# Group statistics summed ahead on ScalarE at the head, and half 1's second modes rewritten

## The chip, the cores and the metric

The kernel runs on one core of a Trainium2 chip. Its metric is the device time of one execution in microseconds (us); of several executions the median counts. Five engines work beside each other, each with an instruction queue of its own: TensorE (PE, with its weight loads as PEld), VectorE (DVE), ScalarE (ACT), GpSimd (POOL) and SyncE (SP). SP only issues DMAs here; ACT and POOL issue some too. Sixteen DMA engines serve the core.

## The reference

Two layers work on x, 256 x 256 pixels of 128 channels in float32; both first normalize x by group statistics and both add their result to x.

```python
x = x + _L0_conv_ref(_gn(x), ...)   # attention along each row of pixels, 4 heads, gated
x = x + _L1_conv_ref(_gn(x), ...)   # 256 tokens of 256 x 128 pixels

def _gn(v, G=32, eps=1e-5):
    g = v.reshape(B_, H_, W_, G, C_ // G)
    m = jnp.mean(g, axis=(1, 2, 4), keepdims=True)
    s = jnp.var(g, axis=(1, 2, 4), keepdims=True)
    return ((g - m) / jnp.sqrt(s + eps)).reshape(v.shape)
```

Layer 0's first normalization needs the mean and variance of all of x before the first row can be computed. Layer 1 attends between tokens and then applies two spectral layers in groups of four tokens: a forward transform of each image to 32 x 16 modes, a complex 4 x 4 mix of the modes with mix_wr and mix_wi, the inverse transform, instance norms, and between the two layers a gelu. What the document calls "second modes" is the part of the second spectral layer that works on modes: transform, mix, energy (for the norm) and the first step of the synthesis.

## The kernel before

**Head (layer0, lines 132 to 171).** A loop over 32 blocks loads x in pieces of 1 MB (tile xb, four buffers, L141), transposes each on PE into PSUM banks (L145; the pool has six) and lets DVE gather bn_stats of each bank (L146). After block 2 the loop asks for the weights (L153), whose transposes stand on PE in the order of the loop; after block 8 comes `prepare` (exponentials of the bias). Then one bn_aggr over all 128 pieces (L166), `group_stats` (L46 to 61: two matmuls with gavg, an evacuation on ACT after each, `rsqrt` with a Sqrt on ACT), and `fold` (L231), which scales the weights wq and wg by the result.

**Rows (Rows.run, L280).** One pass over 256 rows, with an order of PE, ACT, DVE, POOL and SP written out by hand. For a pair of rows `turn` transposes x and kv on DVE (L303) and asks for the pair after next; `project` computes queries and keys (L318 evacuates), `values` the values and the gate's input (L322 to 328), `gates` the tanh. `scores`, two exponentials (L352), a product with the bias on DVE for two heads (L368) and on POOL for the other two (L370), pair sums on POOL (L375), then `attend`. Row 0's projection, values and gate stand before the first scores.

**Half 1's second modes (second_modes with a = 1, L1729).** Tokens are worked on in two halves of 128. `first_images(1)` writes the transformed rows as 16 stores of 16 image rows each to Yd in DRAM, from POOL's queue (L1723). `second_modes` then loads Yd in pieces YT of 512 KB by chunk of modes and half of the rows (L1741), from SP, into two buffers (chunks 2 and 3 wait for 0 and 1); `forward` transforms a chunk (L1754) and copies it to F (L1760); `mix_modes` makes 32 products of 256 elements on DVE and POOL (L1505), each added up by a matmul with the identity (L1518), chunks 0 and 1 first; `mixed` copies the sums to Z; `norm` takes the energies (L1543) and an rsqrt; `synth_modes` makes each of four chunks in four banks (L689), copies them (L707, ACT and DVE in turn) and stores them to Gd2 from SP and ACT (L712), with two gt buffers. Its pools are opened after those of the stage before are closed. Meanwhile `Output1.ahead` loads y and x for four half blocks and sums them (ACT L1907, POOL L1911).

**Output of half 1 (Output1.run, L1913).** For each of 16 blocks: skip and image matmuls (L1322, L1307) from modes `gs` that SP loads from Gd2 (L1331), ACT evacuates (L1843), DVE adds x + y (L1849; for the later half blocks L1896 has made that sum), POOL stores (L1850). SP's queue holds, in this order: modes of four blocks, y and x of half blocks 4 to 7, then for each block the modes four ahead and y and x eight half blocks ahead. There are eight half-block buffers for x and five for y.

Of the kernel before, what the change touches and what calls it, by code (L numbers as in the profile page):

```python
# [10 lines left out]
FP = mybir.dt.float32  # L11
# [19 lines left out]
def rsqrt(nc, pool, out, var, eps, tag):  # L31
# [8 lines left out]
    nc.vector.tensor_mul(n, r, r)  # L40
    nc.vector.tensor_mul(n, n, ve)
# [65 lines left out]
def layer0(tc, I, C, ident, x1d, U, Q2, mv2, groups):  # L107
# [11 lines left out]
    with ExitStack() as ctx:  # L119
# [11 lines left out]
        rows = Rows(tc, I, rctx, x1d, U, Q2, mv2, wT, bg, adft, bad, ident)  # L131
        with tc.tile_pool(name="l0p", bufs=2) as pp, tc.tile_pool(
            name="l0pp", bufs=6, space=PSUM
        ) as ps_p:
            gavg = pp.tile([P, P], FP, name="gavg", bufs=1)
            stats = pp.tile([P, NS // 2, 6], FP, name="stats1", bufs=1)

            xr = x.rearrange("s q c -> (s q) c").rearrange("(b p n) c -> b p n c", p=P, n=16)
            for b in range(xr.shape[0]):
                xb = pp.tile([P, 16, P], FP, tag="xb", name=f"xb_{b}", bufs=4)  # L140
# [6 lines left out]
                if b == 2:  # L147
                    nc.sync.dma_start(gavg, C["gavg"])
                    nc.sync.dma_start(bg, I["L0_conv_bg"].unsqueeze(1))
                    nc.sync.dma_start(adft, C["adft"].rearrange("(j p) f -> p j f", p=P))  # L150
                    for n in ("wq", "wk", "wv", "wg", "wo"):
# [5 lines left out]
                        if n in ("wq", "wo"):  # L157
                            nc.scalar.mul(wT[n], ps[:, 0:P], WO_SCALE if n == "wo" else 1.0 / math.sqrt(32.0))
                        else:
                            nc.scalar.copy(wT[n], ps[:, 0:P])  # L160
                if b == 8:
                    rows.prepare(pp, ps_p)
            rows.load(0)
            rows.load(1)
            mv = pp.tile([P, 2], FP, name="mv1", bufs=1)
            nc.vector.bn_aggr(mv, stats.rearrange("p a b -> p (a b)"))  # L166
            g = group_stats(nc, pp, ps_p, mv, gavg, "g1")
            nc.vector.tensor_copy(mr, g)
            rows.fold(ps_p, mr)

        rows.run()
# [35 lines left out]
class Rows:  # L207
# [23 lines left out]
    def fold(self, psum, mr):  # L231

        nc = self.tc.nc
        nc.vector.tensor_scalar(self.nm, mr[:, 0:1], -1.0, None, ALU.mult)
        ps = psum.tile([P, 512], FP, tag="a", name="foldps")
        for k, n in enumerate(("wq", "wg")):
            nc.vector.tensor_scalar(self.wn[n], self.wT[n], mr[:, 1:2], None, ALU.mult)
            nc.tensor.matmul(ps[:, k : k + 1], self.wn[n], self.nm, start=True, stop=True)
        nc.vector.tensor_copy(self.qb, ps[:, 0:1])
        nc.vector.tensor_scalar(self.hbg, ps[:, 1:2], self.bg, 0.5, ALU.add, ALU.mult)  # L240
# [39 lines left out]
    def run(self):  # L280
# [4 lines left out]
        wk = ctx.enter_context(tc.tile_pool(name="l0wk", bufs=2))  # L285
        ps_s = ctx.enter_context(tc.tile_pool(name="l0s", bufs=1, space=PSUM))
        ps_a = ctx.enter_context(tc.tile_pool(name="l0a", bufs=4, space=PSUM))
        pairs = {}
        turned = wk.tile([P, 6, 512], FP, name="turned", bufs=1)
# [19 lines left out]

        def project(s):  # L310
            p, q = row(s)
            ps = ps_a.tile([P, 512], FP, tag="a", name=f"qk_{s}")
            by_columns(ps[:, 0:256], self.wn["wq"], p["xT"][:, q])
            by_columns(ps[:, 256:512], wT["wk"], p["kvT"][:, q])
            r = rows[s] = {}
            r["qkT"] = wk.tile([P, 512], FP, tag="qkT", name=f"qkT_{s}")

            nc.scalar.activation(r["qkT"], ps, AF.Identity, bias=self.qb)  # L318

        def values(g):  # L320
# [4 lines left out]
            p["v"] = wk.tile([P, 4, P], FP, tag="v", name=f"v_{g}")  # L325
            nc.scalar.copy(p["v"].rearrange("p c d -> p (c d)"), ps)
            p["g"] = ps_a.tile([P, 512], FP, tag="a", name=f"g_{g}")
# [134 lines left out]

        with tc.manual_schedule(engines={ENG.PE, ENG.Activation, ENG.DVE, ENG.Pool, ENG.SP}):
            turn(0)
            for i in range(-1, NS + 1):
# [4 lines left out]
                if not odd and whole(g):  # L470
                    gates(g)
# [4 lines left out]
                if 0 <= i < NS:  # L476
# [3 lines left out]
                    weigh(i)  # L480
                if odd and whole(g + 1):
                    values(g + 1)
                if odd and whole(g + 2):
                    turn(g + 2)
# [151 lines left out]
def layer1(tc, I, C, ident, x1d, upool, U, Q2, groups, out):  # L636
# [9 lines left out]
    with ExitStack() as ctx:  # L646
# [983 lines left out]
        def first_images(a, wp, yp, psk, pst, first=None):  # L1630
# [44 lines left out]
            for b in range(17):  # L1675
# [37 lines left out]
                if b > 0:  # L1713
# [9 lines left out]
                    nc.gpsimd.dma_start(  # L1723
# [4 lines left out]

        def second_modes(a, wp, mk, psum, gts, yts):  # L1729

            h = halves[a]
            ym, yv, ra, lam, r2, rho, sig, _, kap, c0, hm, hv = (h.col[:, k : k + 1] for k in range(12))
# [29 lines left out]
            if a:  # L1762
                for hc in range(2):
                    for c in range(2):
                        load(c, (hc,))

                nc.scalar.activation(h.col[:, 12:13], yv, AF.Sqrt)
            else:
                load(0)
# [3 lines left out]
            load(2 if a else 1)  # L1773
            yield 4.0
            forward(1)
            if not a:
                load(2)
# [14 lines left out]
            for c in range(4):  # L1792
                if c == 2:
                    ps = psum.tile(f"cvps_{a}")
                    for i in range(4):
                        for r in range(2):
# [7 lines left out]
                            queues=(nc.sync if a else nc.gpsimd, nc.scalar))  # L1804
# [4 lines left out]
                if c == 1:  # L1809
                    run(tail)  # L1810

                    for i in range(4):
                        r = slice(32 * i, 32 * i + 32)
                        v = h.row[r, 0:P].rearrange("k (b d x) -> k b d x", b=2, d=2)
                        nc.vector.tensor_tensor(
                            h.bl0[r].rearrange("k (b d x) -> k b d x", b=2, d=2),
                            v[:, :: (-1 if i & 2 else 1), :: (-1 if i & 1 else 1)],
# [364 lines left out]
```

## Time and profile before

| | us |
|---|---|
| median of 3 runs | 2650.92 (2647.06 to 2656.12) |
| profiled execution, its own time | 2650.27 |
| its span on the core | 2648.5 |
| busy in the span: PE / DVE / POOL / ACT | 2406.1 / 2032.0 / 1485.6 / 1420.4 |
| input pass, to the end of the last bn_stats | 0 to 101.1 |
| rows begin: first product on POOL | 123.0 |
| last yA stored, second modes of half 1 begin | 2442.8 |
| last store of modes has landed | 2504.2 |

A line of the profile's timeline has the start, the duration, the engine, the line of the program, the operation, what it writes and reads, shapes, how many, and in brackets how long the engine had been idle before it and what ended that. A line of the chain of waits has start, length and the work that the end was waiting for. In the 40 slices each digit is a busy share in tenths, for PEclk the granted clock of TensorE in tenths.

### The profile page before, as it was taken

To read this page: it belongs to the slowest core of one execution; us is meant where nothing else is said; L and a number is where in the kernel's file an instruction comes from. 1 tells how busy PE (TensorE), PEld (TensorE's weight loads), DVE (VectorE), ACT (ScalarE), POOL (GpSimd) and SP (SyncE) were. 2 spreads that over 40 slices of the span, in tenths; PEclk is the share of its full clock that TensorE was granted. 3 is DMA by queue.
4 is the path that set the end of the run, shared out by engine and by line. 5 is a ranking of instruction groups with operands and counts; after the bars stand their busy time and mean duration, and the time that the engine had idled before them with its cause. 6 is when DMAs were issued, how large, how long until landed. Compare 5 with 4: busy or idle time off the path is not lost. (4 is left out here: it accounts for less than half of the span.)

```text
span 2648.5 us, 88789 instructions
## 1 busy us (share of the span) xinstructions
PE 2406.1 (91%) x37586; PEld 1537.2 (58%) x37586; DVE 2032.0 (77%) x2883; ACT 1420.4 (54%) x2720; POOL 1485.6 (56%) x1041
## 2 busy tenths in 40 slices
PE   6699999999999999999998999998979888898754
PEld 6555655555565656565554567786754466454522
DVE  7799999999999999999997457566646654465455
ACT  0278888888888888888885122001016402555232
POOL 1199999999999999999995012002136412111211
PEclk9899999999999999999998999999989988999855
DMA  9655566566565656566563011888877755997699
GB/s 360 215 92 101 105 107 107 103 107 106 105 106 100 111 100 109 103 106 106 105 107 70 6 58 63 268 273 289 296 278 268 261 194 159 333 349 268 196 384 350
DMA packets 1016869, 458.49 MB, mean 173 GB/s; under 512 B 831062, under 2 KB 946217, under 8 KB 1010072
## 3 DMA queue, kind: packets, MB, share of 16 engines
q1 hardware_dynamic: 976664, 362.61, 54.7%
q0 software_dynamic: 22912, 81.80, 8.0%
q10 hardware_dynamic: 16896, 8.39, 1.1%
q8 instruction: 298, 4.88, 0.8%
q14 instruction: 99, 0.81, 0.1%
HBM read 317.36 MB, written 135.27 MB: 171 GB/s over the span
## 5 line engine op out<-in xcount | busy, mean ns | idle before, releaser
L370 POOL TENSOR_TENSOR e<-e,b1T 128x1024 f32<-128x1024 f32 x255 | 604.4, 2370 | 145.8 <-DMA xk<-in_L_conv_kv_x_dram 78.5
L375 POOL TENSOR_TENSOR es<-e 128x512 f32<-128x512 f32 x512 | 648.0, 1288 | 0.1
L397 DVE RECIPROCAL av<-av 128x256 f32<-128x256 f32 x256 | 452.2, 1766 | 9.1
L352 ACT ACTIVATE sc<-sc,b2T 128x512 f32<-128x512 f32 x514 | 340.0, 662 | 123.9 <-PE sc L343 111.8
L352 ACT ACTIVATE e<-sc,b2T 128x512 f32<-128x512 f32 x510 | 322.8, 693 | 0.0
L368 DVE TENSOR_TENSOR e<-sc,b1T 128x1024 f32<-128x1024 f32 x257 | 312.1, 1215 | 10.1 <-ACT sc L352 9.7
L343 PE MATMUL sc<-qkT 32*128 32x256 f32 x4096 | 293.7, 400 | 2.5 <-DVE e L368 2.5
L1440 PE MATMUL yps<-xt,mpT 128*128 128x256 f32 x1024 | 246.5, 391 | 31.8 <-DMA xt<-x1d 16.0
L385 PE MATMUL av<-e,v 128*32 128x256 f32 x4096 | 268.6, 379 | 1.8 <-DVE gate L398 1.7
L343 PEld LDWEIGHTS sc<-qkT 32*128 32x128 f32 x4096 | 185.7, 184 | 114.9 <-issue 52.3
L1440 PEld LDWEIGHTS yps<-xt,mpT 128*128 128x128 f32 x1024 | 192.0, 193 | 76.1 <-DVE yt L1452 20.2
L385 PEld LDWEIGHTS av<-e,v 128*32 128x32 f32 x4096 | 130.2, 110 | 125.8 <-issue 38.1
L1456 POOL DMA_DIRECT2D yd<-yt x32 | 17.4, 545 | 317.0 <-DVE yt L1452 311.1
L318 ACT ACTIVATE qkT<-qk,qb 128x512 f32<-128x512 f32 x256 | 174.0, 680 | 6.6 <-PE qk L295 6.5
L295 PE MATMUL qk<-turned,wn_wq 128*32 128x256 f32 x2048 | 164.0, 392 | 1.8 <-DVE turned L303 1.8
L442 ACT ACTIVATE turned<-turned 128x256 f32<-128x256 f32 x256 | 104.3, 408 | 112.1 <-DVE x1b L410 109.8
L390 PE MATMUL av<-es,ones 128*32 128x256 f32 x2048 | 160.7, 379 | 1.6 <-POOL es L375 1.6
L295 PEld LDWEIGHTS u<-adft,x 128*32 128x32 f32 x4096 | 118.5, 110 | 74.9 <-issue 74.7
L295 PE MATMUL qk<-turned,wT_wk 128*32 128x256 f32 x2048 | 157.9, 380 | 0.0
L303 DVE STREAM_TRANSPOSE turned<-xk 128x1024 f32<-128x1024 f32 x128 | 157.8, 1233 | 0.1
L1843 ACT ACTIVATE blocks<-h2ps,col 128x512 f32<-128x512 f32 x128 | 88.8, 778 | 128.1 <-PE h2ps L1307 128.1
L295 PE MATMUL u<-adft,x 128*32 128x129 f32 x4096 | 137.0, 273 | 0.0
(544 smaller groups left out, 4163.8 us busy)
## 6 DMA issues: line engine op xcount, KB each, us to landing
xt<-x1d SPq DMA_DIRECT2D x128, 512.0 KB, 6.6
xb<-in_x_dram SPq DMA_DIRECT2D x32, 1024.0 KB, 7.8
xk<-in_x_dram SPq DMA_DIRECT2D x512, 64.0 KB, 3.2
xk<-in_L_conv_kv_x_dram SPq DMA_DIRECT2D x512, 64.0 KB, 2.8
x1d<-x1b SPq DMA_DIRECT2D x512, 64.0 KB, 2.3
x<-x1d SPq DMA_DIRECT2D x126, 256.0 KB, 3.2
y<-yd SPq DMA_DIRECT2D x62, 512.0 KB, 7.1
gs<-Gd SPq DMA_DIRECT2D x384, 64.0 KB, 5.4
```

The source lines that it names most:

```text
L295: nc.tensor.matmul(out[hd], w[:, hd], src, start=start, stop=stop)
L303: nc.vector.transpose(turned[:, a : b + 1 : b - a].rearrange("p k (b c) -> p k b c", c=32), t)
L318: nc.scalar.activation(r["qkT"], ps, AF.Identity, bias=self.qb)
L343: nc.tensor.matmul(sc[h // 2][:, h % 2, c * 256 : (c + 1) * 256], qkT[p, 256 + c * P : 256 + (c + 1) * P], qkT[p, 0:256], start=True, stop ...
L352: nc.scalar.activation(r["e"][1][:, :, c, :] if hp and s < NS - 1 else z, z, AF.Exp, bias=b2T[:, c, s : s + 1])
L368: nc.vector.tensor_tensor(e, sc.rearrange("p h x -> p (h x)"), w, ALU.mult)
L370: nc.gpsimd.tensor_tensor(e, e, w, ALU.mult)
L375: nc.gpsimd.tensor_tensor(es, e[:, :, 0, :], e[:, :, 1, :], ALU.add)
L385: nc.tensor.matmul(ps[hd, 0:256], p["v"][:, 2 * (s % 2) + c, hd], r["e"][h // 2][:, h % 2, c, :], start=(c == 0), stop=(c == 1),)
L390: nc.tensor.matmul(ps[32 * h : 32 * h + 32, 256:512], self.ones, r["es"][h // 2][:, h % 2, :], start=True, stop=True,)
L397: nc.vector.reciprocal(rd, rd)
L1440: nc.tensor.matmul(rows_of(ps[j]), mpT[:, sc, tt], by_turn(xt[:, sc])[:, j], start=(sc == 0), stop=False,)
```

## The change

*Head.* Blocks of x lie in five fixed places inside the tile U (free until the rows fill it) instead of four buffers; the pool of PSUM banks has four. After block 29 the statistics of the first 30 blocks are summed by ACT (three activations with accumulators) and finished by POOL; a Sqrt is issued behind them. After the last block bn_aggr takes only the last two blocks, and the matmuls with gavg add both parts, weighted by 30/32 and 2/32. `rsqrt` has one DVE operation fewer, the evacuations on ACT are gone. `Rows.run` is a generator now: pair 0 is turned and its keys are made before the rsqrt, row 0's queries after the fold of wq, and the gate of pair 0 after the first row's products.

*Half 1's second modes.* A class LastModes takes the place of second_modes(1). All of Yd is loaded into tiles of the pool xp: rows 0 to 127 in two loads, rows 128 to 223 in three, rows 224 to 255 in three. The last yA is stored from ACT's queue. The transforms of the first 128 rows run for all chunks, then those of the second; products are made in 16 groups of two, DVE's straight from PSUM, every third group on POOL, three buffers; PSUM banks are named by use. Synthesis goes 1, 0, 2, 3; all its stores are issued by SP. y and x are loaded for half blocks 0 and 1 ahead of the stores, for 2 and 3 behind the last; the sums are made on DVE.

*Output.* The x tiles hold whole blocks (three in xp, one in op), y has four buffers, gs five. The pools xp and head stay open. Elsewhere `shift` and `turned_blocks` hold what second_modes did in place, for both halves.

```diff
@@ layer0 @@
+steps = rows.run()
+next(steps)
 with tc.tile_pool(name="l0p", bufs=2) as pp, tc.tile_pool(
-    name="l0pp", bufs=6, space=PSUM
+    name="l0pp", bufs=4, space=PSUM
 ) as ps_p:
-    gavg = pp.tile([P, P], FP, name="gavg", bufs=1)
+    gavg = pp.tile([P, 2, P], FP, name="gavg", bufs=1)
...
+    NB, late = xr.shape[0], 2
+    for b in range(NB):
+        xb = room[:, 2048 * (1 + b % 5) : 2048 * (2 + b % 5)].rearrange("p (n c) -> p n c", c=P)
...
+        if b == NB - late - 1:
+            early = stats[:, 0 : 4 * (b + 1)].rearrange("p b (h k) -> p (b h) k", h=2)
+            n, flat = 8 * (b + 1), junk[:, 0 : 8 * (b + 1)]
+            nc.gpsimd.tensor_scalar(col[:, 6:7], early[:, 0, 1:2], -1.0, None, ALU.mult)
+            nc.scalar.activation(flat, early[:, :, 1], AF.Identity, bias=col[:, 6:7], accum_out=col[:, 7:8])
+            nc.scalar.activation(
+                flat, early[:, :, 1], AF.Square, bias=col[:, 6:7], accum_out=col[:, 8:9]
+            )
+            nc.scalar.activation(flat, early[:, :, 2], AF.Identity, accum_out=col[:, 9:10])
+            nc.scalar.activation(col[:, 10:11], col[:, 9:10], AF.Sqrt)
+            g = nc.gpsimd
+            g.tensor_scalar(col[:, 7:9], col[:, 7:9], 1.0 / n, None, ALU.mult)
+            g.tensor_tensor(col[:, 0:1], col[:, 7:8], col[:, 6:7], ALU.subtract)
+            g.tensor_tensor(col[:, 7:8], col[:, 7:8], col[:, 7:8], ALU.mult)
+            g.tensor_scalar(col[:, 9:10], col[:, 9:10], 1.0 / (256 * n), None, ALU.mult)
+            g.tensor_tensor(col[:, 8:9], col[:, 8:9], col[:, 7:8], ALU.subtract)
+            g.tensor_tensor(col[:, 2:3], col[:, 8:9], col[:, 9:10], ALU.add)
...
+    with tc.manual_schedule(engines={ENG.PE, ENG.Activation, ENG.DVE, ENG.Pool}):
+        nc.vector.bn_aggr(last, stats[:, 4 * (NB - late) :].rearrange("p a b -> p (a b)"))
+        nc.vector.tensor_copy(col[:, 1:4:2], last)
+        ps = ps_p.tile([P, 512], FP, tag="a", name="g1_ps")
+        for k in range(2):
+            nc.tensor.matmul(ps[:, 0:1], gavg[:, k], col[:, k : k + 1], start=(k == 0), stop=(k == 1))
+        nc.vector.tensor_copy(mr[:, 0:1], ps[:, 0:1])
+        d = col[:, 4:6]
+        nc.vector.tensor_scalar(d, col[:, 0:2], mr[:, 0:1], None, ALU.subtract)
+        nc.vector.tensor_mul(d, d, d)
+        nc.vector.tensor_add(d, d, col[:, 2:4])
+        ps = ps_p.tile([P, 512], FP, tag="a", name="g1_ps2")
+        for k in range(2):
+            nc.tensor.matmul(ps[:, 0:1], gavg[:, k], d[:, k : k + 1], start=(k == 0), stop=(k == 1))
+        next(steps)
+        rsqrt(nc, pp, mr[:, 1:2], ps[:, 0:1], EPS, "g1")
+        ps = ps_p.tile([P, 512], FP, tag="a", name="foldps")
+        rows.fold(ps, mr, "wq")
+        next(steps)
+        rows.fold(ps, mr, "wg")
+for _ in steps:
+    pass
@@ Rows.run @@
+yield
+turn(0)
+keys(0)
+yield
+project(0)
+yield
+wk = ctx.enter_context(tc.tile_pool(name="l0wk", bufs=2))
+ps_s = ctx.enter_context(tc.tile_pool(name="l0s", bufs=1, space=PSUM))
 with tc.manual_schedule(engines={ENG.PE, ENG.Activation, ENG.DVE, ENG.Pool, ENG.SP}):
-    turn(0)
-    for i in range(-1, NS + 1):
+    values(0)
+    turn(1)
+    for i in range(0, NS + 1):
...
+        if i == 0:
+            gate(0)
+            gates(0)
         if odd and whole(g + 1):
             values(g + 1)
+            gate(g + 1)
@@ layer1: first_images, LastModes @@
-            nc.gpsimd.dma_start(
+            (nc.scalar if a and b == 16 else nc.gpsimd).dma_start(
...
+        self.low = [tile("xt", 3, 1024, f"YT0_{k}") for k in range(2)]
+        for k in range(2):
+            nc.sync.dma_start(self.low[k], rows[0:P, :, 1024 * k : 1024 * k + 1024])
+        self.high = [tile("yt", 2, 512, f"YT1_{k}") for k in range(2)] + [tile("xt", 3, 1024, "YT1_2")]
+        at = (slice(0, 512), slice(512, 1024), slice(1024, 2048))
+        for lo, hi in ((0, 96), (96, P)):
+            for t, c in zip(self.high, at):
+                nc.sync.dma_start(t[lo:hi], rows[P + lo : P + hi, :, c])
...
+        for f in range(4):
+            (nc.vector.tensor_copy if engines[f] else nc.scalar.copy)(gt[:, f, :], banks[f])
+        for ri in range(2):
+            for jp in range(2):
+                k = 2 * ri + jp
+                r0 = 16 * ri + 4 * c
+                nc.sync.dma_start(
+                    halves[1].Gd2[r0 : r0 + 4, 2 * jp : 2 * jp + 2].rearrange("f j g t -> (j g) f t"),
+                    gt[:, :, k * P : (k + 1) * P],
+                )
@@ LastModes.run @@
+        for hc in range(2):
+            for c in range(4):
+                for r in range(2):
+                    for k in range(2):
+                        for f in range(4):
+                            nc.tensor.matmul(
+                                fw[c // 2][32 * f : 32 * f + 32, c % 2, r, :],
+                                efwd[:, hc, (2 if r else 1) if k else 0, :],
+                                self.spectrum(c, hc, 1 - r if k else r, f),
+                                start=(hc == 0 and k == 0 and r == 0 and c % 2 == 0), stop=(hc == 1 and k == 1 and r == 1 and c % 2 == 1),
+                            )
...
+        def group(k, n):
+            made = xp.tile([P, 2, 2, G, 4], FP, tag="gs", name=f"z1m_{k}_{n}", bufs=3)
+            pool = n % 3 == 2
+            for q in range(2):
+                i, (x, r, dst) = n // 2, ((0, "r", 0), (1, "n", 0), (0, "i", 1), (1, "r", 1))[2 * (n % 2) + q]
+                src = F[:, 2 * k : 2 * k + 2] if pool else fw[k]
+                f = src[:, :, x, :].rearrange("p c (g i) -> p c g i", i=4)[:, :, :, i]
+                w = mixw[r][:, 2 * k : 2 * k + 2, 16 + 4 * i : 20 + 4 * i]
+                (nc.gpsimd if pool else nc.vector).tensor_tensor(
+                    made[:, q], bc(f, 3, 4), bc(w, 2, G), ALU.mult
+                )
+            for q in range(2):
+                nc.tensor.matmul(
+                    acc[k][:, n % 2].rearrange("p c t -> p (c t)"), ident,
+                    made[:, q].rearrange("p c g o -> p (c g o)"), start=(n == 0 and q == 0),
+                    stop=(n == 7 and q == 1),
+                )
...
+        for n in range(8):
+            group(0, n)
+        for r in range(2):
+            nc.scalar.copy(Z[:, 1, r, :], acc[0][:, r, 1])
+        nc.scalar.activation(Z[:, 0, 0, :], acc[0][:, 0, 0], AF.Identity, scale=z0)
+        nc.scalar.activation(Z[:, 0, 1, :], acc[0][:, 1, 0], AF.Identity, scale=wsyn[:, 0:1])
+        squares(0)
+        gt0 = gts(0)
+        o1.load(0)
+        o1.load(1)
+        for n in range(3):
+            group(1, n)
+        self.synth(1, four(1), gts(1), (0, 0, 0, 0))
+        nc.scalar.activation(F[:, 0], F[:, 0], AF.Identity, scale=hw0)
+        for n in range(3, 8):
+            group(1, n)
+        o1.add(0)
+        nc.scalar.copy(Z[:, 2:4, 0, :], acc[1][:, 0])
+        nc.vector.tensor_copy(Z[:, 2:4, 1, :], acc[1][:, 1])
+        self.synth(0, four(0), gt0, (0, 1, 0, 1))
+        squares(1)
+        o1.add(1)
+        self.synth(2, four(2), gts(2), (0, 1, 0, 1))
...
+        rsqrt(nc, op, rs, en[:, 0:1], EPS, "rq")
+        dg = op.tile([P, P], FP, tag="m", name="z1dg", bufs=2)
+        nc.vector.scalar_tensor_tensor(left, en[:, 0:1], EPS, rs, ALU.add, ALU.mult)
+        nc.vector.tensor_scalar(dg, ident, left, None, ALU.mult)
+        nc.vector.tensor_mul(left, rs, rs)
+        nc.vector.tensor_mul(left, left, en[:, 0:1])
+        self.synth(
+            3, [bank("f", 2, "g21gp_3_0")] + [bank("acc", 2, f"g21gp_3_{f}") for f in (1, 2)]
+            + [bank("s", 4, "g21gp_3_3")], gts(3), (0, 1, 0, 1),
+        )
+        o1.load(2)
+        o1.load(3)
+        nc.tensor.matmul(en[:, P : 2 * P], ones, dg, start=True, stop=True)
+        h.row = en[:, P : 2 * P]
@@ Output1 @@
-        old = k < 5 or k % 5 < 2
-        y = (self.wp if old else self.more).tile(
-            [P, HB], FP, tag="yo", name=f"y4_{k}", bufs=2 if old else 3
+        b = k // 2
+        if k % 2 == 0:
+            self.blocks[b] = (
+                self.op.tile([P, NB], FP, tag="gt", name=f"w1_{b}", bufs=1) if b % 4 == 3
+                else xp.tile([P, NB], FP, tag="xt", name=f"w1_{b}", bufs=3)
+            )
+        y = (
+            self.op.tile([P, HB], FP, tag="ya", name=f"y4_{k}", bufs=2) if k >= 4 and k % 4 < 2
+            else xp.tile([P, HB], FP, tag="yt", name=f"y4_{k}", bufs=2)
         )
         nc.sync.dma_start(y, ydv[:, 1, px])
-        x = (self.wp if k % 8 < 5 else self.more).tile(
-            [P, HB], FP, tag="xo", name=f"x4_{k}", bufs=5 if k % 8 < 5 else 3
-        )
+        x = self.blocks[b][:, k % 2 * HB : k % 2 * HB + HB]
...
-            gs[b] = (self.wp if b % 4 < 2 else self.more).tile(
-                [P, 4, P], FP, tag="gs", name=f"gs3_1_{b}", bufs=2
+            gs[b] = (
+                self.op.tile([P, 4, P], FP, tag="m", name=f"gs3_1_{b}", bufs=2) if b % 5 > 2
+                else xp.tile([P, 4, P], FP, tag="gs", name=f"gs3_1_{b}", bufs=3)
             )
             load_modes(gs[b], halves[1].Gd2, b)
         for b in range(4):
             modes(b)
+        self.add(2)
+        self.add(3)
@@ end of layer1 @@
     pz.release_now()
-    with tc.tile_pool(name="op1", bufs=2, side="right") as op:
-        o1 = Output1(op)
-        with tc.tile_pool(name="mp3", bufs=1) as wp, tc.tile_pool(
-            name="mpq3", bufs=8, space=PSUM
-        ) as psq:
-            m1 = second_modes(1, wp, tiles(wp), Banks(psq, "q"), [(wp, "gt", 2)], [(wp, "gt", 2)] * 4)
-            next(m1)
-            o1.more = op
-            ahead = o1.ahead()
-            next(ahead)
-            next(ahead)
-            next(m1)
-            next(m1)
-            next(ahead)
-            next(ahead)
-            run(iter(lambda: next(m1), 1.2))
-            run(ahead)
-            run(m1)
-        with tc.tile_pool(name="opk1", bufs=8, space=PSUM) as psk, tc.tile_pool(
-            name="op2", bufs=1
-        ) as more:
-            o1.run(Banks(psk, "k"), more)
+    op = ctx.enter_context(tc.tile_pool(name="op1", bufs=1))
+    o1, last = Output1(op), LastModes(op)
+    last.load()
+    with tc.tile_pool(name="mpq3", bufs=1, space=PSUM) as psq:
+        last.run(psq, o1)
+    with tc.tile_pool(name="opk1", bufs=8, space=PSUM) as psk:
+        o1.run(Banks(psk, "k"))
```

## The prediction

> **What bounds the kernel now.** I read four views in this order: the page's busy shares in 40 slices (one slice is 66.2 us), the timeline of the head, the chain of waits over the last 230 us, and the windows of the output stage.
>
> ```profile
> PE   6699999999999999999998999998979888898754
> PEld 6555655555565656565554567786754466454522
> DVE  7799999999999999999997457566646654465455
> ACT  0278888888888888888885122001016402555232
> POOL 1199999999999999999995012002136412111211
> PEclk9899999999999999999998999999989988999855
> DMA  9655566566565656566563011888877755997699
> ```
>
> DVE and POOL are at nine tenths in slices 3 to 20, the stage of the attention rows; in slices 37 to 40 PE falls from 8 to 4 while DMA climbs to 9. So the ends of the kernel have limits of their own, and the change touches only these ends. The timeline of the head:
>
> ```profile
> 101.16 3.62 DVE L166 BATCH_NORM_AGGREGATE mv<-stats 128x2 f32<-128x768 f32 x1
> ...
> 107.18 1.28 ACT L37 ACT_TABLE_LOAD   x1
> ...
> 111.78 2.37 DVE L303 STREAM_TRANSPOSE turned<-xk 128x1024 f32<-128x1024 f32 x2
> ...
> 122.97 2.36 POOL L370 TENSOR_TENSOR e<-e,b1T 128x1024 f32<-128x1024 f32 x1 [78.50 <-DMA xk<-in_L_conv_kv_x_dram]
> ```
>
> The last bn_stats ends at 101.13; everything up to POOL's first product at 122.97 is one serial chain, 21.84 us. POOL's next product (127.78) starts 4.81 later, and a row costs POOL 2.36 + 2.53 (L370 and the two L375): POOL paces the rows from the first one on. A start of POOL that is earlier by d ends the stage earlier by d. The chain of waits at the tail:
>
> ```profile
> 2446.26 4.57 DMA YT<-Yd
> ...
> 2454.30 8.88 DMA YT<-Yd
> ...
> 2500.00 4.21 DMA Gd<-g21gt
> ...
> 2512.88 5.75 DMA x<-x1d
> ```
>
> After the last write of Yd has landed (2446.1) the modes take until 2504.2: two pairs of YT loads in turn, mixing until 2482.2 (Z's copy on DVE), four syntheses and stores until 2504.2. Then come 16 loads of modes, and at 2512.5 the loads of y and x. The output stage's windows (length, then busy us of PE, PEld, DVE, ACT, POOL; clock, DMA share, GB/s):
>
> ```profile
> 2500.00:2520.00 20.00, 14.05 (x288) 7.51 (x258) 5.52 (x16) 10.31 (x17) 1.14 (x2) 0.74 0.72 213
> 2520.00:2540.00 20.00, 4.79 (x64) 2.83 (x64) 9.60 (x9) 3.59 (x6) 2.13 (x4) 0.63 1.03 391
> ```
>
> From 2520 to 2620 the DMA share is 1.03 at 380 to 397 GB/s: the output is DMA-bound, its bytes are unchanged, so it ends earlier by as much as its stream starts earlier.
>
> **Head, the serial chain.** s is the end of the last bn_stats. bn_aggr took 3.62 for 768 elements and 1.89 for 384 (L1770), so 4.5 ns an element; the 48 of the last two blocks cost 0.38, the copy into the columns 0.2: s+0.6 instead of s+3.65. Matmul, evacuation and three column operations keep their 1.5 (104.78 to 106.27): s+2.1. The second matmul, now two, 1.1; beside it DVE turns pair 0 (1.23), so ve is at s+3.6, about 0.3 later than the matmul asks. Sqrt starts at once: the 1.28 table load at 107.18 goes, as an earlier Sqrt has loaded it. Reciprocal and three operations (one fewer, about 0.2) give mr at s+4.6, written in place (the copy L168, 0.2, goes). wn_wq, nm, the fold matmul, qb: s+5.9, as before (109.65 to 111.56, less what wn_wg now does later). The keys are done meanwhile; queries 1.08, qkT 0.69: s+7.5, where it was s+14.8 (115.90). PE then has the fold of wg, the values (1.97) and the scores, ACT the values' copy (0.6) and the exp table's 1.28: first exp at about s+11.2. From the first exp to POOL's product took 3.25 (119.72 to 122.97): s+14.5. **Gain 7.3**; bounds 5 (PE's half clock, 0.50 here, on every matmul, and a late second pair) and 8.5 (table load hidden). The gate's matmul and tanh (1.97 and 0.69) come after the first row's products, beside POOL's 4.9; without that cover they cost 2.7 once.
>
> The sums of the first 30 blocks: four ACTIVATEs with their accumulator reads (0.2 to 0.6 each), one table load 1.28, seven small POOL operations (memsets of 128x1 took 0.1, a 128x128 one 0.28), in all about 4 us. They lie beside the eight last bn_stats, 8 x 0.62 = 5.0 (19 took 11.80); without that cover up to 2 us. The one matmul that waits for them stands on PE behind no transposes.
>
> **Head, the input pass.** Five 1 MB buffers for four, four PSUM banks for six. DVE waited 1.75 for the last block (98.11), and 7.5 at 15 to 22 while PE waited for weights wv to wo, whose loads stand behind SP's waits; blocks 30 to 95 run at 415 to 424 GB/s with DVE full as well. An earlier request can give back the 1.75 and up to 1.2 more; a weight load queued behind one more block (2.5 us) can cost that much, fewer banks about 0.5. Between -3 and +3; I take **+1.0**, near the 1.75 row.
>
> **Tail, up to the modes.** The last yA is copied at 2442.5. Its store moves from POOL's queue (3.3 us to landing) to ACT's, where the nearest stores took 4.2 to 5.6 beside others; I take 3.3: 2445.8. Behind the issue on ACT (0.5) stand only a table load and a Sqrt that nobody needs yet. All other YT data (2 MB of rows 0 to 127, 96 of the other 128 rows) is asked for ahead, while DMA has a share of 0.56 (2420 to 2440). Only 32 rows, 0.5 MB, remain: between the 2.8 of a 64 KB transfer to 32 partitions (xk) and the 4.57 of the pair above; I take 3.6: 2449.4. The pair of 8.88 is off the path.
>
> [...] No row here has 0.5 MB on 32 partitions.
>
> The first 128 rows' transforms of all chunks run at 2442.6 to 2446.7; the second rows' are half of 4 x 1.96 (64 records at clock 1.0): 3.9, or 7.3 at clock 0.50 (64 took 3.64 at 2450.9). I take 4.6: 2454.0.
>
> In this trace PE sat idle from 2443.3 to 2450.9 and ran at 0.50 until 2455. [...]
>
> **Tail, modes and stores.** Mixing becomes PE's: 16 groups of four records, 1.15 each (2475.08), against 0.86 on DVE (2 x 0.43) and one group in three on POOL (1.72 with 3.4 to give). 8 x 1.15 gives 2463.2, three groups 2466.7, synthesis 1 (2.07) 2468.7, five groups 2474.5, synthesis 0 2476.5, a wait of 1.0 for its copies, synthesis 2 2479.6, the energies 1.95, synthesis 3 2483.6. Its DVE copies stand behind the 2.6 of the rsqrt chain (2487.5 to 2490.1 now): 2485.5; four issues of 0.42 on SP and 4.2 to landing: **2491.0 for 2504.2, gain 13.2**. Bounds 5 and 16. The two adds on DVE (1.28 each, for ACT 1.15 and POOL 2.37 now) lie under PE's last groups and syntheses; uncovered they cost 1.3 each, since Z's copy or synthesis 2's copies queue behind them. y and x for 0 and 1 (2 MB, some 6 us) are in long before; for 2 and 3 they follow the last stores, so nothing delays those, but the first modes arrive behind them, about 1 us late and not in the DMA's way.
>
> **Output.** Now SP stalls 2.9 at y6 on the add of y4 (DMA 213 GB/s in 2500 to 2520). Then four y buffers are free, so 4 MB go out at once: at most 2.7. Against it, a w tile holds two halves, so a slot returns with the later store: should block 2 get block 0's slot, some 5 are lost. Between -5 and +2.7; I take **+1.0**.
>
> **Sum.** 7.3 + 1.0 + 13.2 + 1.0 = 22.5. The profiled execution took 2650.27 (span 2648.5 and 1.77 around it), 0.65 under the median 2650.92: 2650.3 - 22.5 = 2627.8, so 2628, which the median agrees with.
>
> **Rivals.** *The modes are not PE's (0.18).* Now a mixing half took 11.3 (2470.9 to 2482.2); at that pace both take 22.6 for 18.4, the half clock costs 2.7, a slow reload 1, an uncovered add 1.3: tail gain 4, 2650.3 - 9.3 - 4 - 1 = 2636. For it: PE waited for POOL and DVE products in this stretch. Against: three buffers for two, and POOL is rid of four adds. *The input pass pays (0.08).* Weights queue behind 1 to 2 more blocks and DVE idles 5 more: head gain 2 to 3, 2633. *Both, or the early requests do nothing (0.06).* A gain of 4 to 6: 2645. *Slower (0.06).* The slot of two halves makes the x load of block b+4 wait for both stores of block b. Now a store lands 7.5 after its issue and the load follows 1.7 to 3.4 later; if that slack turned to less than -2.6, each of 12 blocks would lose that, and 12 x 2.6 = 31 eats the gain of 22.5 and 8 more. It decides from there: 2659. Against: SP there waits for its own queue (33.7 and 24.9 us on x and y), not for slots.
>
> The forecast itself has 0.62. About 8 us (0.3%) is what a measurement can tell here. Faster 0.88, same 0.06, slower 0.06. The range runs from the good ends of the four terms (8.5 + 3 + 16 + 2.7 = 30.2: 2620) to between rivals one and three: 2620 to 2643.
>
> **What would show it.** Right: POOL's first L370 product at 113 to 116; bn_aggr under 0.5; no YT load on the chain after 2450; the last Gd store landed near 2483 (8.3 of head taken off), the loads of y4 some 8 after it and a DMA share of 1.0 from there. Wrong: POOL's pace after the first row over 4.9, PE idle between mixing groups, SP waiting for out stores at the x loads, or bn_stats ending after 101.

## The result, and the profile after

Six executions of the changed kernel took 2633.34 us in the median (2628.53 to 2637.42), six of the kernel before, on the same chip, 2653.07 (2647.06 to 2656.12): ratio 0.9928, 95% interval 0.9913 to 0.9942, a gain of 19.7 us. The forecast was 2628, a gain of 22.5 on 2650.3, and the range 2620 to 2643. So time and sign were right; one of the four terms had the wrong sign, by 6 us, and another was too small by 2 to 4. That the gain came within 3 us of the forecast is luck in that part.

Single executions of the same code differ by 10 to 20 us, so the comparison goes by stretches of the profiled executions, cut at the same five events. In us ("chain": last bn_stats to POOL's first product; "middle": from the last row to the last yA copy, where the edits only take one DVE operation out of each rsqrt; "modes": from there to the issue of the first load of modes; "output": to the end of the span). That issue stands 0.2 to 1.4 us ahead of the landing of the last Gd2 store (2504.8 in the kernel before, whose 2504.2 is the landing of the store before it):

| profile of | input pass | chain | rows | middle | modes | output | span |
|---|---|---|---|---|---|---|---|
| before | 101.1 | 21.8 | 1308.4 | 1011.1 | 61.7 | 144.3 | 2648.5 |
| before, again (e4) | 100.9 | 21.5 | 1309.5 | 1012.1 | 63.3 | 144.7 | 2651.9 |
| head alone (e1) | 98.8 | 14.3 | 1308.4 | 1019.1 | 63.9 | 146.0 | 2650.5 |
| tail alone (e2) | 97.7 | 21.6 | 1308.4 | 1018.8 | 46.5 | 149.6 | 2642.6 |
| after | 99.5 | 14.7 | 1308.4 | 1017.2 | 46.3 | 149.5 | 2635.7 |
| after, again (e3) | 99.1 | 14.6 | 1308.4 | 1016.1 | 45.5 | 149.3 | 2633.1 |

The middle spreads by 8 us over these rows with nearly the same code (by 16 over all fourteen profiles): that is the noise in the totals. It is longer where TensorE's granted clock is lower: 1011.1 at a mean of 0.953 over the middle (before), 1019.1 at 0.945 (e1), 1027.1 at 0.942 (e6), a correlation of -0.75 over the fourteen. So the totals of the two profiles differ by only 12.8; without the middle their stretches differ by 18.9, near the 19.7 of the medians. The other columns repeat to about 1 us, the input pass to 3.

The head in the timeline after the change:

```profile
99.52 0.37 DVE L192 BATCH_NORM_AGGREGATE mv<-stats 128x2 f32<-128x48 f32 x1
...
110.64 1.36 ACT L404 ACTIVATE sc<-sc,b2T 128x512 f32<-128x512 f32 x2
...
114.14 2.36 POOL L422 TENSOR_TENSOR e<-e,b1T 128x1024 f32<-128x1024 f32 x1 [16.41 <-ACT e L404]
```

bn_aggr takes 0.37 for 3.62, the first exponential begins 11.2 after the last bn_stats (99.48), POOL's first product 14.7 after it. The chain of waits over the tail (start, length, what was waited for):

```profile
2439.86 3.73 DMA Yd<-yA
2443.68 3.59 DMA YT<-Yd
...
2447.31 6.51 PE f1ps L1970 x128
2453.82 9.69 PE z1acc L1998 x44
...
2486.15 8.15 DMA gs<-Gd
2494.35 2.35 PE h2ps L1372 x21
```

Only one reload is left on the chain; the transforms behind it took 6.51, eleven mixing groups 9.69. The first modes then arrive 8.15 after they are asked for. The whole output stretch in the windows (length, busy us of PE, PEld, DVE, ACT, POOL; clock, DMA share, GB/s), of before:

```profile
2504.20:2648.50 144.30, 76.24 (x992) 45.36 (x992) 72.30 (x60) 44.30 (x64) 17.10 (x32) 0.59 0.93 350
```

and after the change:

```profile
2486.20:2635.70 149.50, 79.55 (x992) 48.09 (x992) 75.45 (x66) 44.38 (x64) 17.15 (x32) 0.58 0.94 351
```

The last column times the length is the number of bytes: 350 x 144.3 = 50.5 MB, 351 x 149.5 = 52.5 MB. The rate is the same and 2 MB have come in: the loads of y and x for half blocks 2 and 3, four of 512 KB. That fits the 5 us by which this stretch is longer; e5 and e6 below test it.

### The profile page after: what moved, and what is told of

Same layout as the page of the kernel before. It is cut to its first block, busy times and chain, and to the rows that moved or that the text cites. A ratio compares the mean times of both kernels' runs of the same rounds, so it can differ in the third digit from the quotient of the medians.

```text
span 2635.7 us, 88777 instructions
## 1 busy us (share of the span) xinstructions
PE 2418.5 (92%) x37590; PEld 1546.8 (59%) x37590; DVE 2024.6 (77%) x2872; ACT 1422.7 (54%) x2732; POOL 1476.0 (56%) x1043
## 5 line engine op out<-in xcount | busy, mean ns | idle before, releaser
L337 PE MATMUL qk<-turned,wT_wk 128*32 128x256 f32 x2048 | 164.5, 393 | 0.4 <-DVE g_ve L35 0.4
L337 PE MATMUL qk<-turned,wn_wq 128*32 128x256 f32 x2048 | 157.9, 380 | 0.0
L2086 POOL DMA_DIRECT2D out_dram<-w x64 | 34.3, 536 | 186.6 <-DVE w L2085 186.4
```

The source lines that it names most:

```text
L337: nc.tensor.matmul(out[hd], w[:, hd], src, start=start, stop=stop)
```

## The experiments

**One part alone, and both kernels again.** Four kernels on one chip, beside the kernel before (2654.19, 23 executions). e1 has the edits of layer0, Rows and rsqrt only, e2 those of layer1 only; e3 and e4 are the two kernels unchanged.

```diff
 e1: head alone
+    NB, late = xr.shape[0], 2
+    rows.fold(ps, mr, "wq")
...
 e2: tail alone
+    o1, last = Output1(op), LastModes(op)
+    last.load()
```

> Only the head of the change, the tail as before. In the profile of the whole change POOL's first product of the rows starts 8.8 earlier than before, the rows' end 8.8, but the last copy of yA only 2.7. Theory A, the loss in between is spread from one execution to the next: this kernel gains about 9 in time (2644 beside 2653), POOL's first product at 114 and the rows' end near 1421. Rival B, the head's gain is taken back in the middle by something the change does: a gain of 2 to 4 (2649 to 2651), the loss in the same place in the profile.

Measured: 2651.83 (10 executions), ratio 0.9976 [0.9952, 1.0]; chain 14.3 for 21.5 to 21.8, nothing else shorter beyond the input pass's own spread. The 9 us of theory A did not appear in the time: a gain of 2.4, not clear of none, which is rival B's number, with a middle of 1019.1.

> Only the tail of the change (half 1's second modes and output), the head as before. By the profiles of before and of the change, the stretch from the last copy of yA to the last landed store of modes is 15.4 shorter and the output after it 5.3 longer. Theory A: a gain of about 10 in time (2643 beside 2653), and the two stretches again near 46.3 and 149.6. Rival B, the tail is worth all that was measured (some 20) and the head nothing: 2633. Rival C, pools kept open cost the middle 6: the loss is seen here before the last copy of yA, gain 4.

Measured: 2639.72 (7), ratio 0.9946 [0.9924, 0.9968], a gain of 14.5; modes 46.5, output 149.6, as theory A has them.

> The changed kernel once more, for a second profile of it. Theory A, the loss of 6.2 between the rows' end and the last copy of yA is spread: it is a different number here, between 0 and 6, and goes with this execution's own time (2628 to 2637). Rival B, it belongs to the change: it is 6 again.

Measured: 2634.91 (5), ratio 0.9915 [0.9884, 0.9945].

> The kernel before once more, for a second profile. Theory A: the stretch from the rows' end to the last copy of yA differs by several us from the 1012.4 of the first profile, with the execution's own time (2647 to 2656). Rival B: it is within 1 us of it.

Measured: 2653.26 (10), ratio 0.9995 [0.9975, 1.0015].

The two parts add: 0.9976 x 0.9946 = 0.9922, beside 0.9915 and 0.9928 for both. The tail's gain in the modes and its loss in the output are both there without the head. The middle of these first profiles looks like rival B's: 1011.1 and 1012.1 in the two of the kernel before, 1016.1 to 1019.1 in the four with edits. But of the eight later profiles, all with both parts, seven have 1012.1 to 1014.6 and one (e6) 1027.1. That speaks against the edits as the cause, though no profile of the kernel before was taken on their chips; the clock goes with part of the difference, and the rest stays open.

**Where the output's 5 us come from.** e5 moves the four loads for half blocks 2 and 3 behind the first sixteen loads of modes; e6 leaves them out.

```diff
 e5                                    e6, in Output1.load
-                o1.load(2)           +if k in (2, 3):
-                o1.load(3)           +    nc.gpsimd.memset(y, 0.0)
...                                   +    nc.gpsimd.memset(x, 0.0)
+                self.load(2)         +else:
+                self.load(3)         +    (the two loads)
```

> The loads of y4 and x for half blocks 2 and 3 (2 MB) move from ahead of the first sixteen loads of modes to behind them, on the same queue; nothing else changes. The output stretch (last Gd2 store landed to the end of the span) is 149.5, 149.3 and 149.6 us in the three profiles with the new tail, 144.3 to 146.0 with the old one. Theory A, bytes: GB/s times length gives 52.5 MB for the new stretch and 50.5 MB for the old one; the 2 MB were loaded in the modes' stretch before and now stand in a stretch that is full, 2 MB / 0.39 GB per ms = 5.1 us. Their place in the queue is then without weight: the first image comes some 6 us earlier, but the stretch stays at 149 to 150. Theory B, order: the first modes land 8.2 us after their issue because they queue behind the 2 MB, and the images start late for it. The stretch then falls to 145 to 146.

> This kernel leaves out the four loads of y4 and x for half blocks 2 and 3 (2 MB): POOL fills those tiles with zeros in their place, so two of the 32 half blocks of the second half's output lack their inputs. Theory A, bytes: the output stretch falls from 149.5 to 149.5 - 5.1 = 144.4, to within 1 us, the length it had with the old tail. Rival: the stretch is set by the chain modes, image, add, store and not by the bytes: it falls by under 2, to 147.5 or more. Were it the queue order alone (theory B), it would fall to 145 to 146 here as in the run with the modes first; the two runs together tell A from B.

Measured: e5 148.8, e6 143.5, one execution each. SP's queue in the timeline of e5, and the landing of the first modes in its chain of waits:

```profile
2483.43 8.12 SPq L1396 DMA_DIRECT2D gs<-Gd  x16
2491.59 0.42 SPq L2127 DMA_DIRECT2D y<-yd  x1
```

```profile
2483.43 2.43 DMA gs<-Gd
```

The sixteen issues took 8.12 for 12.00, and the first modes landed 2.43 after their request, for 8.15. So the first image came 5.7 us earlier in its stretch (2.5 for 8.2 after the first load of modes was issued), and the end only 0.7. In the output windows of e5 and e6 the rate is unchanged:

```profile
2483.40:2632.20 148.80, 80.51 (x992) 49.15 (x992) 75.91 (x71) 44.37 (x64) 17.10 (x32) 0.59 0.94 354
2495.60:2639.10 143.50, 79.89 (x992) 48.16 (x992) 76.04 (x71) 44.35 (x64) 17.10 (x32) 0.56 0.94 352
```

e6 differs from e5 by the bytes (and POOL's zeros) and is 5.3 shorter; 2.1 MB (four times 512 KB) at 390 GB/s (377 to 393 in the windows of 2520 to 2620 after the change) are 5.4: theory A, bytes. The order took off 0.7. The cut moves a little with it, as the first load of modes no longer stands behind four issues on SP: counted from the start of the mixing to the end of the span, e5 took 180.4, e6 175.1 and five profiles with the change's order 181.7 to 182.6, so the order is worth up to 1.6 and the bytes again 5.3. Order is cheap here since the DMA engines (a share of 0.94 over the stretch), and not the images (PE busy for 80.5 of 148.8 us), are what the stretch is short of.

**The input pass.** e7 gives the staging tile of the projection weights five buffers.

```diff
-w = pp.tile([P, P], FP, tag="w", name="w_" + n)
+w = pp.tile([P, P], FP, tag="w", name="w_" + n, bufs=5)
```

> The staging tile of the five projection weights in the input pass gets five buffers for two, so no weight load waits for a transpose of an earlier one, and no block load stands on SP behind such a wait. In the profile after the change DVE idles 9.8 us at 14.8 to 24.6 while PE waits for weights (4.88 and 3.11 us). Theory: that idle time is the weights' and goes; the last bn_stats then ends 3 to 5 us earlier, at 94.5 to 96.5 for 99.1 to 99.5, and the kernel takes 3 to 5 us less (2629 to 2632 beside 2634). Rival 1: the stretch is bound by the loads' rate: in blocks 30 and later 415 to 424 GB/s with DVE full, so what the early gap gives is lost at the next wait for a block; last bn_stats at 98 to 99.5, gain under 1.5. Rival 2: the gap is the weight loads' own queueing behind block loads, and stays at 8 to 10 us.

Measured: 2633.86 (4 executions), ratio 0.9915 [0.9882, 0.9949], the same as e3's: in the time no gain shows. DVE in the timeline after the change:

```profile
24.57 0.70 DVE L151 BATCH_NORM_STATS2 stats<-xps 128x6 f32<-128x512 f32 x1 [9.77 <-PE xps L150]
```

and in e7:

```profile
17.05 1.44 DVE L151 BATCH_NORM_STATS2 stats<-xps 128x6 f32<-128x512 f32 x2 [1.97 <-PE xps L150]
```

The idle 9.77 becomes 1.97, so it was the weights' wait for their two buffers. But only part of these 7.8 us reaches the end of the pass: the last bn_stats ends at 96.6, and at 97.2 and 96.7 in the two later kernels with this edit, for 99.0 in the mean of the eight profiles with the new head and two buffers (98.3 to 99.8). 2.2 us: between the theory (3 to 5) and rival 1. DVE then idles elsewhere (6.4 us for 2.7 after 30 us), the longest 3.98 at 37.0, while PE makes the transposes of `prepare`.

**The pause ahead of the second transforms.** e9 fills it with work nobody reads.

```diff
+if hc:
+    warm = bank("s", 4, "warm")
+    for i in range(4):
+        nc.tensor.matmul(warm, ident, self.low[0][:, 0, 0:512], start=(i == 0), stop=(i == 3))
```

> Four matmuls of 128x512 into a bank that nobody reads stand on PE between the transforms of the first 128 rows and those of the second: some 4 x 0.89 = 3.6 us at the pace of the mixing groups (0.44 for 256 columns), in the 3.65 us in which PE waited for the reload. In the profile after the change the second transforms took 6.51 us, at a granted clock of 0.50 in 2447.3 to 2450.0 and 0.61 in 2450 to 2454, and 4.6 had been priced. Theory: the clock fell in the pause and the transforms pay for it: with PE busy they take 3.6 to 4.2 (half of what 256 records take at clock 1.0), the clock stays over 0.9 in that window, and the stretch from the last yA copy to the last Gd2 store is 43 to 44.5 for 45.5 to 46.5. Rival: the transforms are slow for another reason (32 rows of data arriving, weight loads): they stay above 5.5.

Measured: modes 45.0, one execution 2635.13. PE's timeline:

```profile
2441.61 3.70 PE L1969 MATMUL warm<-YT,ident 128*128 128x512 f32 x8
2446.05 1.95 PE L1974 MATMUL f1ps<-YT,k_efwd 128*32 128x128 f32 x64 [0.74 <-DMA YT<-Yd]
2448.26 1.95 PE L1974 MATMUL f1ps<-YT,k_efwd 128*32 128x128 f32 x64 [0.26 <-DMA YT<-Yd]
...
2473.67 2.65 PE L1936 MATMUL g21gp<-z1Z,k_esyn 32*128 32x128 f32 x64
```

and its window over the transforms:

```profile
2446.05:2450.20 4.15, 3.89 (x129) 3.42 (x129) 1.42 (x4) 0.59 (x1) 1.19 (x2) 1.00 0.63 205
```

The transforms run in 2 x 1.95 at a granted clock of 1.00, as the theory says: the fallen clock was the price, 1.1 to 2.6 us over 3.9. The stretch hardly gains, for two reasons in the same lines. Now PE waits for the last piece of the reload (2448.26), which it had been too slow to notice; and in this run the clock falls in synthesis 3 (2.65 for 2.07; the last section comes back to it). So the theory holds for the transforms and failed for the stretch (43 to 44.5 expected).

**The reload in one piece.** e8 takes the split of 96 and 32 rows back.

```diff
-for lo, hi in ((0, 96), (96, P)):
+for lo, hi in ((0, P),):
```

> The last 128 rows of Yd are reloaded in one piece (2 MB) once the last yA is stored, where the change reloads 96 of them ahead and 32 (0.5 MB) behind that store. In the six profiles with the split the time from the landing of the store to the first transform of the second rows is 3.1 to 4.4 us. Theory: the split pays, as only the bytes behind the last store count: the piece of 2 MB takes 7 to 8 at the rates of this stretch, PE's pause grows from 4 to 8, and the stretch from the last yA copy to the last Gd2 store grows from 45.0 to 48 to 50. Rival: 32 partitions load at a lower rate per byte than 128, and the split saves under 1.5: stretch 45 to 46.5.

Measured: modes 49.0, one execution 2635.67. The chain of waits:

```profile
2441.32 7.80 DMA YT<-Yd
...
2449.16 2.89 PE f1ps L1970 x64
```

From the store's landing (2439.83) the reload took 9.3. Of the split reload the first of three pieces is in after 3.6, the second after 4.4 and 5.2 (e7, e11), the last after 6.2 (e9), and PE begins with the first. PE's pause grew to 5.85 only, not to 8, as it begins with the first piece here too. Per byte the 32 rows did come slower than the 128, as the rival has it (0.5 MB in 6.2, 2 MB in 9.3), but the stretch is 3.4 longer than the 45.5 in the mean of six profiles with the split, which therefore pays.

**The 2 MB back into the modes' stretch.** e10 loads x for half blocks 2 and 3 ahead of synthesis 1's stores and y4 between the later stores; e11 adds the edits of e7 and e9; e12 is e10 with the edit of e7 and the last y4 behind all stores.

```diff
-    ... if c % 2
+    ... if c in (1, 2)          # gt buffer of op: syntheses 1 and 2
 o1.load(1)
+o1.load_x(2)
+o1.load_x(3)
...
 self.synth(0, four(0), gt0, (0, 1, 0, 1))
+o1.load_y(2)
...
 self.synth(2, four(2), gts(2), (0, 1, 0, 1))
+o1.load_y(3)                    # e12: behind synthesis 3
...
-o1.load(2)
-o1.load(3)
```

> The 2 MB of y4 and x for half blocks 2 and 3 are loaded within the modes' stretch again, as the old tail did: x behind the loads for 0 and 1, y4 for 2 behind the stores of synthesis 0, y4 for 3 behind those of synthesis 2. For the room, synthesis 2 goes through the buffer of synthesis 1 and synthesis 3 through that of synthesis 0. Theory (bytes): the output stretch falls from 149.5 to 144 to 146, and the modes' stretch, 45 us at a DMA share of 0.54, grows by no more than the 1.3 us that 0.5 MB ahead of the last stores take: 45 to 46.5; net 3 to 5 us less than the run of the change. Rival: the loads delay the stores by as much as they save (or a buffer that is shared is late): modes 48 to 50, net under 1.

> Three edits to the changed kernel together: five buffers for the projection weights (2.7 us earlier end of the last bn_stats measured), four matmuls in PE's pause (0.8 to 1.7 us earlier start of the mixing measured, of which at most 0.5 stayed), and the inputs of half blocks 2 and 3 loaded early (3 to 5 expected). If the terms add: 2.7 + 0.4 + 4 = 7 us under the run of the change, 2634 - 7 = 2627, ratio to the kernel before 0.990. Rival: the input pass's gain is lost again further on, as the rest of the kernel varies by several us, and the early loads push the last stores: 2631 to 2634, no difference from the change that can be measured.

> Five buffers for the projection weights and early inputs, without the four matmuls in PE's pause, and with y4 for half block 3 behind the stores of synthesis 3 in place of ahead of them. With the early inputs the last Gd2 store took 5.1 and 5.7 us to land behind that y4 (2.7 to 2.9 without it), and the modes' stretch 47.0 and 48.1 for 45; SP also stood 1.5 at that load. Theory: the modes' stretch falls to 45.5 to 46.5 and the output takes the 0.5 MB back, 143.5 + 1.3 = 144.8 (143.5 and 145.0 measured): sum 190.3 to 191.5 for 191.6 and 192.0, so 0.5 to 1.5 less in these two, and 2626 to 2627 in all. With the weights' 2.7 that is 7 to 8 under the kernel of the change, ratio to the kernel before 0.989. Rival: the order is again without weight, as it was for the loads ahead of the first modes: sum of both stretches 191.6 to 192, 2627 to 2628.

| | input pass | chain | modes | output | span | median | ratio to before |
|---|---|---|---|---|---|---|---|
| e10 | 98.6 | 15.0 | 48.1 | 143.5 | 2625.8 | 2627.57 (1) | |
| e11 | 97.2 | 15.1 | 47.0 | 145.0 | 2625.4 | 2627.12 (6) | 0.9891 [0.9867, 0.9914] |
| e12 | 96.7 | 15.0 | 46.2 | 143.1 | 2623.0 | 2625.75 (6) | 0.9907 [0.9889, 0.9924] |

e10's output is 6 us shorter, as theory A has it; the modes lose 2.6 of it, more than the 1.3 expected (48.1 is the lower end of the rival's range), and net 3 to 4 stay. The loss in e10's chain of waits:

```profile
2474.24 1.52 SPq L2144
...
2477.14 5.11 DMA Gd<-g21gt
```

SP stood at y4's load, and the store that the first modes wait for landed 5.11 after its issue, behind that load's bytes. e11's sum of 2627 came out (2627.12). With this load behind the stores (e12) the modes are back at 46.2 and the output does not grow: the theory was right on the modes, and the 1.3 that it charged to the output did not appear. By stretches e12 is 8.2 us under the change (input pass and chain 2.2, modes and output 6.0, against the means of after and e3), by medians 7.6 (2625.75 for 2633.34, on another chip), by the ratios to the kernel before on the same chip 5.6; the intervals of the ratios still overlap. In its profile and its median e12 is the fastest kernel here, by the ratio e11 is; the two cannot be told apart.

## Why the prediction was right, and where it was not

**Head chain, 7.3: right.** 21.8 became 14.7 in the two profiles first compared, 7.2 (6.9 in the means of 3 and 11 profiles). The steps hold as well: mr written 4.6 after the last bn_stats (104.1), qkT done at 7.5, the first exponential at 11.2, POOL at 14.7 for s+14.5. The gate's matmul and tanh hid beside POOL's row, whose products still follow 4.83 apart.

**Input pass, 1.0: not told from none.** The old pass ended at 97.7 to 101.1 in three profiles, the new one at 98.3 to 99.8 in eight: 0.9 in the means, less than the spread. The rival "the input pass pays" had its mechanism: DVE's wait for weights grew from 6.3 to 7.5 in three profiles to 8.3 to 9.8 in eight. It did not cost 5, because DVE makes up for most of an early gap before the end, as e7 shows from the other side (7.8 less idle, 2.2 earlier).

**Tail modes, 13.2: mechanism right, size too small.** 15.4 between the first two profiles, 17.4 in the means (63.0 of three, 45.5 of six). The terms: store 3.73 for 3.3 (ACT's stores around it took 3.2 to 6.0 in the trace of before, not 4.2 to 5.6) and reload 3.59 for 3.6, both near; the transforms 6.5 for the 4.6 taken, too little by 1.9; and, the other way, the mis-sized term, the mixing groups. They ran at 9.76 for eleven, 0.89 each, where 1.15 was charged: 16 x 0.26 = 4.2 too much. The 1.15 is one piece of four records in the old chain of waits at 2475.08; the timeline has 28 records in 7.10 there, 1.01 for four, so my price was above even that row's mean, and the row itself lies in a stretch in which PE still waited for products. Now PE runs the groups back to back, and the pace is that of the matmuls alone: 0.22 for each of four records. Whether the third buffer did this, or the products made straight from PSUM, was not tried apart.

**Output, +1.0: wrong, -5.** The failed step is "the output is DMA-bound, its bytes are unchanged". The first half is right and makes the second half expensive. I had seen that the loads for half blocks 2 and 3 follow the last stores, and charged them for their place in the queue (1 us on the first modes), and not for their 2.1 MB, which the modes' stretch had carried at a DMA share of 0.55 (2460 to 2504). At 390 GB/s they are 5.4; e6 beside e5 measures 5.3. e12 carries them in the modes' stretch again and is 5.4 shorter from the start of the mixing to the end (176.6, for a mean of 182.0 in five profiles with the change's order). A gain from the four y buffers is not seen; they were not tried alone. The w slots behaved: in the whole stretch one x load waited for a store, 1.6 us.

The errors cancel: +4.2 on the modes' side, -6 on the output's. The rivals: "the modes are not PE's" fell (PE is busy without a gap in both mixing stretches), "slower by w slots" did not occur.

**The pause and the clock.** By the prediction's own times PE's pause is 2449.4 - 2446.7 = 2.7 us, and the 4.6 for the transforms behind it lies between 3.9 at full clock and 7.3 at 0.50. Nine profiles with the new tail and no filling have pauses of 3.61 to 5.85 us, and in all of them the transforms behind are slowed (4.98 to 6.53, where the first 128 rows' took 3.70). After the change the granted clock was 0.50 for 6.83 us, from 2446.28 to 2453.11. These 6.83 us in two halves, with as long a piece before and behind (columns as above):

```profile
2442.87:2446.28 3.41, 0.78 (x31) 0.51 (x20) 2.04 (x3) 0.00 (x0) 0.00 (x0) 1.00 0.24 76
2446.28:2449.70 3.42, 2.39 (x48) 2.21 (x52) 0.00 (x0) 0.00 (x0) 0.00 (x0) 0.50 0.27 87
2449.70:2453.11 3.41, 3.41 (x72) 3.15 (x68) 1.42 (x4) 0.59 (x1) 1.19 (x2) 0.50 0.83 288
2453.11:2456.52 3.41, 3.41 (x37) 2.90 (x30) 1.50 (x4) 0.59 (x1) 0.00 (x0) 1.00 0.85 328
```

In the first line PE is busy for 0.78 us, until the pause begins at 2443.65; the clock falls 2.6 us later, stays at 0.50 for 5.80 us of the transforms, and is back at 1.00 for the last of them. With the pause filled (e9) it was 1.00 over all of them. The two kernels with the filling left PE idle for 0.74 and 0.25 us ahead of these transforms, the nine without it for 3.61 and more: how long a pause may be for the clock to stay was not shown. The pause was 1 us longer than predicted because the first transforms took 3.70 for 4.1 and the store 0.4 more.

**The reload.** I took 3.6 for the 32 rows. 3.59 is what the chain shows, but that is the first of the three pieces (128 KB of 512); the last landed 6.2 after the store in e9, the one run in which PE waited for it. So for the whole the 3.6 was 2.6 too little, and the order of the transforms by chunk hid the rest while the clock was low.

## What to carry to other kernels

When a stage is bound by the rate of transfers, count the bytes of the stage before and after (rate times length in the windows), and charge every load that a change moves into it at the full rate, wherever it stands in the queue (here 5.3 us for the bytes and at most 1.6 for the place); a load moved out of a stage with idle DMA has lost a nearly free ride (here a stage at a DMA share of 0.55; with 1.5 of the 2 MB back in it, e12, it took 46.2 for 45.5). A buffer saved in one stage is paid for in the next when it was the prefetch that lived in it. Size a pace from a stretch in which the engine has no gaps at all, and look for waits that a merged row hides.

## What was not expected of the hardware

The granted clock fell while PE was busy. In both kernels with the filled pause (e9, e11) it fell in synthesis 3, and PE had not been idle for over 0.8 us since the first transforms. The windows of e9:

```profile
2470.00:2473.50 3.50, 3.50 (x75) 3.38 (x73) 2.25 (x3) 1.14 (x3) 0.00 (x0) 1.00 0.77 223
2473.50:2476.20 2.70, 2.70 (x67) 2.51 (x66) 1.61 (x9) 0.20 (x1) 0.00 (x0) 0.78 0.98 289
```

Synthesis 3 took 2.65 there and 3.67 in e11 (granted 0.54), and 2.07 in the nine profiles without the filling. Ahead of it stand 1.95 us of energies, matmuls with one column each. The filling is not needed for it: e1, with the old tail and no filling, shows the same fall (the energies, then the windows before and behind the fall):

```profile
2484.97 1.95 PE L1608 MATMUL z1ens<-om,z1sq 128*128 128x1 f32 x16
```

```profile
2484.82:2488.24 3.42, 3.42 (x72) 3.28 (x71) 2.14 (x7) 1.28 (x3) 0.22 (x1) 1.00 0.28 77
2488.24:2491.65 3.41, 3.41 (x36) 3.19 (x31) 3.18 (x12) 1.07 (x2) 0.00 (x0) 0.50 0.85 235
```

Nor do the energies alone bring it about: in the kernel before and in that of the change the same 1.95 us stand ahead of a synthesis (energies at 2485.58 and 2475.40), the clock stays at 1.00 behind them, and the synthesis takes 2.07. What decides was not shown; no run moves the energies alone.
